# The expert stage of a two-layer decoder: transposed residual, Strassen's scheme for the first and last products, routing weights on h

## The chip, the cores and the metric

The kernel runs on one core of a Trainium2 chip. The metric is the device time of one execution in microseconds (us). Engines: TensorE (PE; its weight loads are PEld), VectorE (DVE), ScalarE (ACT), GpSimd (POOL) and SyncE (SP, which issues most of the DMAs).

## The reference, cut to what matters

The decoder has two layers of attention, cross-attention and feed-forward on 8 x 112 = 896 tokens of width 512. The change lies in the last stage, the feed-forward of the second layer, two rounds of experts on the normalized stream:

```python
res = xt                                   # 896 x 512, after the layer norm
for j in range(2):
    gate = xt @ Wg[j] + bg[j]              # 8 gates; the 6 largest count
    w = softmax(where(in_top, gate, -inf))
    h = einsum('th,nhe->nte', xt, Wup) + bup        # 6 experts, 512 -> 256
    h = silu(einsum('nte,nef->ntf', h, Wsw) + bsw) * h
    eo = einsum('nte,neh->nth', h, Wdn) + bdn       # 256 -> 512
    out = einsum('nth,tn->th', eo, w[:, :6])
    sh = (xt @ Wsu + bsu).reshape(-1, 2, 256)       # 2 shared experts
    sh = silu(sh @ Wsa + bsa) * sh
    out = out + sh.reshape(-1, 512) @ Wsd + bsd
    xt = res + out
return x + xt
```

The weights are the same in both rounds; only the gates differ. All is float32.

## The kernel before, in words

The whole program is unrolled. TensorE's instructions stand in the order in which the code writes them (`manual_schedule`); the order on the other engines and on the DMA queues is worked out by a scheduler from priorities and modelled times, and each engine then takes its own queue in order, waiting on semaphores.

The stage is `ffn_1` (from L1307). The layer norm writes `res` (token tiles of 128 x 512); GpSimd adds `res` onto `x` (L1335), so that `x` already holds stream and residual. For each round `j` the seven token tiles are turned by TensorE (`turned_tile`, L314) into `xT`, two halves of 448 tokens with the features on the partitions. For each of eight experts `m` (0 and 1 the shared ones):

- `rise` (L1407), the first product: for two halves of tokens and two blocks of 128 outputs, four products over the 512 features into a PSUM bank of tag `mm`; ScalarE adds the bias into `h1` (L1417).
- `switch` (L1421), the middle product: two products a block, ScalarE's silu (L1433), and GpSimd's product with `h1` into `h` (L1434).
- `down` (L1436), the last product: for each of seven token tiles two products with tokens on the rows and all 512 outputs as columns, into a bank of tag `s`. VectorE then multiplies the PSUM tile by the token's routing weight and adds it to the running sum in one operation (L1447); for shared experts it only adds (L1445).

The order is written out: first product of expert m+1, middle product of m, last product of m−1. The gates (`route`, L1337) are woven between the products of the first experts; `weights` makes the routing weights on VectorE (L1355 to L1389), and `turn` (L1391) turns them, split in two parts for precision, for the product with the experts' last biases (`bd`), which joins the last product of expert 1. The last products of expert 7 in round 0 are woven with the turning of round 1's tiles. At the end each tile of `x` leaves as soon as its sum is complete (L1502).

PSUM has eight banks: two of tag `mm`, two pairs of tag `s` (`wide`), two of tag `t` (`turning`). `wpool` has six slots of 1 MB for weights, in turn used by all stages. Nearly all products go through one helper, `accumulate` (L233), so they carry its line, L235; the tile's name tells them apart (`pf` for the first and the middle product, `po` for the last).

Of the kernel before, what the change touches and what calls it, by code (L numbers as in the profile page):

```python
# [27 lines left out]
_CONSTS = {}  # L28


def _constants():
# [28 lines left out]
    def rows(a):  # L60
# [7 lines left out]
        "ident": np.eye(P, dtype=f),  # L68
        **rope(0, e0, 64),
# [3 lines left out]
        "before": before,  # L73
# [82 lines left out]
def decoder(ctx: ExitStack, tc: tile.TileContext, i: dict, out: bass.AP):  # L156
# [32 lines left out]
    consts = cpool.tile([P, i["consts"].shape[1]], F32, name="consts")  # L189
    nc.scalar.dma_start(out=consts[:, :P], in_=i["consts"][:, :P])  # L190
# [8 lines left out]
    nc.sync.dma_start(out=consts[:, P:], in_=i["consts"][:, P:])  # L199
    first.append(weight(i["a_kv"][1], "wv0"))  # L200
    rspans, n = _spans(_ROWS)
    rows = cpool.tile([P, n], F32, name="rows")
    nc.sync.dma_start(out=rows, in_=i["rows"].partition_broadcast(P))

    def const(name, parts=P):
        at, n = _CONSTS[name]
        return consts[:parts, at : at + n]
# [12 lines left out]
    ctxT = cpool.tile([P, NB, T], F32, name="ctxT")  # L220
# [1086 lines left out]
    def ffn_1():  # L1307
        with (
# [3 lines left out]
            res = rpool.tile([P, NT, D], F32, tag="res", bufs=1, name="res")  # L1312
            nxt = rpool.tile([P, NT, D], F32, tag="nxt", bufs=1, name="nxt")
            up = [weight(i["f_up"][g], f"fup_{g}") for g in (3, 0, 1, 2)]
            dn = [weight(i["f_dn"][g], f"fdn_{g}", *((pool, "dn", 2) if g in (1, 2) else ())) for g in (3, 0, 1, 2)]
            sw = pool.tile([P, 7, 2, 256], F32, tag="sw", bufs=1, name="sw")
            nc.sync.dma_start(out=sw.rearrange("p a b c -> p (a b c)"), in_=i["f_sw"])
            wg = rpool.tile([P, 2, NC, 8], F32, tag="wg", bufs=1, name="wg")
            nc.sync.dma_start(out=wg.rearrange("p a b c -> p (a b c)"), in_=i["f_g"])


            b4 = pool.tile([P, D], F32, tag="b4", bufs=1, name="b4")
# [7 lines left out]
            nc.gpsimd.memset(w4, 0.0)  # L1330
            for tiles in GROUPS:
                layernorm([x[:, k, :] for k in tiles], [res[:, k, :] for k in tiles], eps5, f"ff1_{tiles[0]}", stats_behind[0])
            for k in range(NT):
                with tc.issue_after(spread[0]):
                    nc.gpsimd.tensor_tensor(x[:, k, :], x[:, k, :], res[:, k, :], ALU.add)  # L1335

            def route(j, xT, kept):  # L1337


                def gates(k):  # L1340
                    if k == 0:
                        kept["pg"] = turning(f"pgate_{j}")
                    pg = kept["pg"]

                    for hf in range(2):
                        lo, hi = max(k * P, hf * HT), min((k + 1) * P, (hf + 1) * HT)
                        if lo < hi:
                            accumulate(
                                pg[lo - k * P : hi - k * P, 8 * k : 8 * k + 8],
                                [(xT[hf][:, c, lo - hf * HT : hi - hf * HT], wg[:, j, c, :]) for c in range(NC)],  # L1350
                            )
                    if k == NT - 1:
                        weights(pg)

                def weights(pg):  # L1355
# [3 lines left out]
                        row("bg", P)[:, 8 * j : 8 * j + 8].unsqueeze(1).to_broadcast([P, NT, 8]), ALU.add,  # L1359
# [24 lines left out]
                    kept["w"] = w  # L1384
                    top4 = rpool.tile([P, NT, 8], F32R, tag="top4", name=f"top4_{j}")
                    nc.vector.tensor_copy(top4, w)
                    for at in (0, 64):
                        nc.vector.tensor_copy(w4[:, :, at : at + 8], top4.bitcast(F32))
                        nc.vector.tensor_tensor(w4[:, :, at + 32 : at + 40], w, top4.bitcast(F32), ALU.subtract)  # L1389

                def turn():  # L1391
                    kept["wT"] = wT = rpool.tile([P, NT * P], F32R, tag="wT", bufs=1, name=f"wT_{j}")
                    for a, b in ((0, 4), (4, NT)):
                        pt = turning(f"pwT_{j}_{a}")
                        for k in range(a, b):
                            nc.tensor.transpose(pt[:, (k - a) * P : (k - a + 1) * P], w4[:, k, :], ident)
                        nc.scalar.copy(wT[:, a * P : b * P], pt[:, : (b - a) * P])

                return gates, turn

            def expert(j, m, xT, src, dst, kept):

                g, e, shared = m // 2, m % 2, m < 2
                nm = f"{j}_{m}"
                at, hs = {}, {}

                def rise(hf, between=lambda: None):  # L1407
                    if hf == 0:
                        at["h1"] = pool.tile([P, 2, NB * T], F32, tag="h1", name=f"h1_{nm}")
                    for c in range(2):  # L1410
                        if c:
# [3 lines left out]
                        accumulate(ps[:, :HT], [(up[g][:, k, col0 : col0 + P], xT[hf][:, k, :]) for k in range(NC)])  # L1415
                        bias = col("bsu", 2 * e + c) if shared else col("bup", 2 * (m - 2) + c)
                        nc.scalar.activation(  # L1417
                            at["h1"][:, c, hf * HT : (hf + 1) * HT], ps[:, :HT], AF.Identity, bias=bias
                        )

                def switch(hf):  # L1421
                    if hf == 0:
                        at["h3"] = pool.tile([P, 2, NB * T], F32, tag="h3", bufs=3, name=f"h3_{nm}")
                    tokens = slice(hf * HT, (hf + 1) * HT)
                    for c in range(2):
                        ps = mm(f"pf2_{nm}_{hf}_{c}")
                        wi = 6 if shared else m - 2
                        accumulate(
                            ps[:, :HT], [(sw[:, wi, k, c * P : (c + 1) * P], at["h1"][:, k, tokens]) for k in range(2)]
                        )  # L1430
                        s = rpool.tile([P, HT], F32, tag="silu", name=f"silu_{nm}_{hf}_{c}")
                        bias = col("bsa", c) if shared else col("bsw", 2 * (m - 2) + c)
                        nc.scalar.activation(s, ps[:, :HT], AF.Silu, bias=bias)  # L1433
                        nc.gpsimd.tensor_tensor(at["h3"][:, c, tokens], s, at["h1"][:, c, tokens], ALU.mult)  # L1434

                def down(k):  # L1436
                    po = wide(f"po_{nm}_{k}")[:, 0, :]
                    tokens = slice(k * P, (k + 1) * P)
                    pairs = [(at["h3"][:, c, tokens], dn[g][:, 2 * e + c, :]) for c in range(2)]
                    if m == 1:  # L1440
                        pairs.append((kept["wT"][:, tokens], bd))
                    accumulate(po, pairs)
                    d = dst[:, k, :]
                    if shared:
                        nc.vector.tensor_tensor(d, src[:, k, :] if m == 0 else d, po, ALU.add)  # L1445
                    else:
                        nc.vector.scalar_tensor_tensor(d, po, kept["w"][:, k, m - 2 : m - 1], d, ALU.mult, ALU.add)  # L1447

                return rise, switch, down

            with tc.manual_schedule(engines={mybir.EngineType.PE}):
                tail = []
                for j in range(2):
                    src, dst, base = (res, nxt, res) if j == 0 else (nxt, x, x)
                    xT, kept = new_halves(f"ff1_{j}"), {}
                    experts = [expert(j, m, xT, base, dst, kept) for m in range(8)]
                    gates, turn = route(j, xT, kept)

                    for k in range(NT):
                        if k + 2 < len(tail):  # L1460
                            tail[k + 2]()
                        turned_tile(src[:, k, :], xT, k, f"ff1_{j}")
                        if k == 4:
                            experts[0][0](0)

# [6 lines left out]

                    experts[0][0](1, gate)
                    gate()
                    for m in range(8):
                        rise, switch, down = experts[m]
                        if m + 1 < 8:
                            experts[m + 1][0](0, gate)
                            gate()
                            switch(0)  # L1480
                            gate()
                            experts[m + 1][0](1, gate)
                            gate()
                            switch(1)
                        else:
                            switch(0)
                            switch(1)
                        if m == 1:
                            turn()
                        if m:  # L1490
                            for k in range(NT):
                                experts[m - 1][2](k)
                    tail = [lambda k=k, d=experts[7][2]: d(k) for k in range(NT)]
                    for step in tail[: 2 if j == 0 else NT]:
                        step()

# [3 lines left out]
    flat = out.rearrange("b t d -> (b t) d")  # L1500
    for k in range(NT):
        nc.sync.dma_start(out=flat[k * P : (k + 1) * P, :], in_=x[:, k, :])  # L1502
# [17 lines left out]
```

## Time and profile before

| | |
|---|---|
| runs | 1851.69, 1850.88, 1850.89 us; median 1850.89 |
| span of the profiled execution | 1850.4 us (no other time of that execution is given) |
| expert stage's products | from 1341.3 to 1846.0 us |
| busy: PE, PEld | 1809.1 (98%), 979.2 us |
| busy: DVE, ACT, POOL | 784.2 (42%), 658.1, 591.4 us |
| granted TensorE clock | 0.999 |
| DMA | 108.68 MB in all |

The page gives busy times as shares of the whole span. A matmul row's mean is the time of one record on its own; records overlap, so the pace is read from the chain or the timeline, where merged pieces show a start, a length and a count. A float32 product is two records. `min/median/max` on a single line's answer is in ns. Of the page's forty slices the last eleven hold the expert stage; in them VectorE is one to three tenths busy.

### The profile page before, as it was taken

To read this page: it belongs to the slowest core of one execution; us is meant where nothing else is said; L and a number is where in the kernel's file an instruction comes from. 1 tells how busy PE (TensorE), PEld (TensorE's weight loads), DVE (VectorE), ACT (ScalarE), POOL (GpSimd) and SP (SyncE) were. 2 spreads that over 40 slices of the span, in tenths; PEclk is the share of its full clock that TensorE was granted. 3 is DMA by queue.
4 is the path that set the end of the run, shared out by engine and by line. 5 is a ranking of instruction groups with operands and counts; after the bars stand their busy time and mean duration, and the time that the engine had idled before them with its cause. 6 is when DMAs were issued, how large, how long until landed. Compare 5 with 4: busy or idle time off the path is not lost.

```text
span 1850.4 us, 19741 instructions
## 1 busy us (share of the span) xinstructions
PE 1809.1 (98%) x7088; PEld 979.2 (53%) x7088; DVE 784.2 (42%) x1382; ACT 658.1 (36%) x1954; POOL 591.4 (32%) x520
## 2 busy tenths in 40 slices
PE   8999999999999999999999999999999999999999
PEld 4454544545554555677655555545554444554444
DVE  5455666655454545786432323336811112121213
ACT  2444344454333334565232322347632111121120
POOL 3455555355556530000233443302411011021111
PEclk9999999999999999999999999999999999999999
DMA  6132423043242212021212121301020000000001
GB/s 238 26 121 77 129 84 127 18 148 109 51 137 54 50 40 91 24 91 46 88 42 71 38 83 26 139 0 47 24 87 0 1 0 0 0 1 0 1 0 40
DMA packets 35497, 108.68 MB, mean 59 GB/s; under 512 B 6644, under 2 KB 20012, under 8 KB 28744
## 3 DMA queue, kind: packets, MB, share of 16 engines
q1 hardware_dynamic: 28264, 77.97, 13.0%
q0 software_dynamic: 6848, 29.36, 5.3%
q8 instruction: 56, 0.92, 0.2%
q14 instruction: 41, 0.34, 0.1%
q10 hardware_dynamic: 288, 0.09, 0.0%
HBM read 78.83 MB, written 10.22 MB: 48 GB/s over the span
## 4 chain that ended last, share of the span: by engine, by line
PE 89%; DVE 6%; ACT 3%; DMA 1%; SPq 1%; issue 0%; POOL 0%; POOLq 0%; DVEq 0%; ACTq 0%
PE pf L235 16%; PE po L235 11%; PE pr_q L235 10%; PE po_at L370 5%; PE po_at L374 5%; PE po_x L852 4%; PE pv L235 3%; PE ps L619 3%; PE po L637 3%; PE pr_k L235 3%; PE po_x L370 2%; PE pq_x L235 2%; PE po_x L374 2%; PE ps_x L816 2%; PE po_ff L1093 2%; PE ph L235 2%
## 5 line engine op out<-in xcount | busy, mean ns | idle before, releaser
L235 PE MATMUL pr_q<-xT_at,wq 128*128 128x448 f32 x512 | 204.1, 543 | 0.0
L1434 POOL TENSOR_TENSOR h<-silu,h 128x448 f32<-128x448 f32 x64 | 72.8, 1137 | 408.4 <-ACT silu L1433 408.4
L235 PE MATMUL pf<-xT_ff,fup 128*128 128x448 f32 x512 | 199.8, 541 | 1.6 <-ACT xT_ff L322 1.6
L235 PE MATMUL po<-fdn,h 128*128 128x512 f32 x448 | 197.2, 592 | 0.0
L235 PEld LDWEIGHTS pf<-xT_ff,fup 128*128 128x128 f32 x512 | 96.0, 190 | 93.0 <-issue 87.2
L404 POOL TENSOR_TENSOR p<-p,total 112x896 f32<-112x896 f32 (+1 forms) x56 | 85.4, 1531 | 179.4 <-DVE total L400 150.1
L1417 ACT ACTIVATE h<-pf,cols 128x448 f32<-128x448 f32 x64 | 40.6, 634 | 280.7 <-PE pf L235 278.2
L235 PEld LDWEIGHTS pr_q<-xT_at,wq 128*128 128x128 f32 x512 | 93.5, 190 | 84.6 <-issue 78.7
L235 PEld LDWEIGHTS po<-fdn,h 128*128 128x128 f32 x448 | 84.6, 190 | 100.6 <-issue 100.1
L397 ACT ACTIVATE p<-p,nmax 112x113 f32<-112x113 f32 x256 | 95.8, 376 | 109.2 <-DVE nmax L394 108.5
L370 PE MATMUL po_at<-wo,oT 128*128 128x512 f32 x224 | 109.9, 613 | 0.0
L374 PE MATMUL po_at<-wo,oT 128*128 128x512 f32 x224 | 105.3, 592 | 0.0
L235 PE MATMUL pf<-h,sw 128*128 128x448 f32 x256 | 101.5, 540 | 0.0
L567 POOL TENSOR_TENSOR qT<-qT,turned_q 128x448 f32<-128x448 f32 x64 | 75.6, 1185 | 53.9 <-DVE turned_q L566 47.4
L975 POOL TENSOR_SCALAR tl<-tr,ternary_bounds 128x512 f32<-128x512 f32 x32 | 51.8, 1617 | 122.8 <-DMA tr<-in_c_w_dram 122.8
L852 PE MATMUL po_x<-pT_x,kv 125*128 125x448 f32 x192 | 89.3, 549 | 1.7 <-DVE pT_x L847 1.4
L822 DVE TENSOR_REDUCE nmax_x<-ps_x 112x2 f32<-112x750 f32 x64 | 57.1, 933 | 79.5 <-PE ps_x L816 79.5
L565 POOL TENSOR_TENSOR qT<-raw_q,consts 128x448 f32<-128x448 f32 x64 | 79.7, 1251 | 26.1 <-ACT raw_q L556 18.7
L824 ACT ACTIVATE p_x<-ps_x,nmax_x 112x375 f32<-112x375 f32 x124 | 69.8, 575 | 38.2 <-DVE nmax_x L822 38.1
L416 DVE COPY pT<-ppt 112x448 f32<-112x448 f32 x96 | 57.0, 615 | 61.0 <-PE ppt L415 60.9
L1447 DVE SCALAR_TENSOR_TENSOR nxt<-po,wr,nxt 128x512 f32<-128x512 f32 x42 | 31.5, 751 | 120.6 <-PE po L235 120.6
L1447 DVE SCALAR_TENSOR_TENSOR x<-po,wr,x 128x512 f32<-128x512 f32 x42 | 31.5, 751 | 118.8 <-PE po L235 118.8
(255 smaller groups left out, 3189.1 us busy)
## 6 DMA issues: line engine op xcount, KB each, us to landing
tw<-in_c_w_dram SPq DMA_DIRECT2D x16, 512.0 KB
tr<-in_c_w_dram POOLq DMA_DIRECT2D x32, 256.0 KB, 4.1
signs<-tl POOLq DMA_DIRECT2D x32, 256.0 KB, 2.9
turned_q<-raw_q SPq DMA_DIRECT2D x128, 56.0 KB
turned_q<-raw_q SPq DMA_DIRECT2D x64, 112.0 KB
wq<-in_a_q_dram SPq DMA_DIRECT2D x4, 1024.0 KB
wo<-in_a_o_dram SPq DMA_DIRECT2D x4, 1024.0 KB
bq<-in_b_q_dram SPq DMA_DIRECT2D x4, 1024.0 KB
```

The lines of the kernel that those rows point to most:

```text
L235: nc.tensor.matmul(ps, lhsT, rhs, start=(k == 0), stop=(k == len(pairs) - 1))
L370: nc.tensor.matmul(ps[0], lhsT, rhs, start=(c == 0), stop=False)
L374: nc.tensor.matmul(ps[0], lhsT, rhs, start=False, stop=(c == len(pairs) - 1))
L397: nc.scalar.activation(p[:, h, :], src[:, h, :], AF.Exp, bias=nmax[:, h : h + 1], accum_out=total[:, h : h + 1])
L404: spread[:] = [nc.gpsimd.tensor_tensor(p[:, at, :T], p[:, at, :T], total[:, at], ALU.mult).ins]
L565: nc.gpsimd.tensor_tensor(by_batch(dst), by_batch(raw), cos, ALU.mult)
L567: nc.gpsimd.tensor_tensor(dst, dst, turned, ALU.add)
L822: nc.vector.tensor_reduce(nmax, ps[:T, :, :L], AX.X, ALU.max, negate=True)
L824: e = nc.scalar.activation(p[:, 2 * j + s, :], ps[:T, s, :L], AF.Exp, bias=nmax[:, s : s + 1], accum_out=total[:, 2 * j + s : 2 * j + s + 1],)
L852: nc.tensor.matmul(po[0][:, : 4 * T], kv[:, b, c, :], pTs[c], start=(c == 0), stop=(c == NLC - 1))
L1434: nc.gpsimd.tensor_tensor(at["h3"][:, c, tokens], s, at["h1"][:, c, tokens], ALU.mult)
L1447: nc.vector.scalar_tensor_tensor(d, po, kept["w"][:, k, m - 2 : m - 1], d, ALU.mult, ALU.add)
```

## The change

All of it is for the last stage, with some room made for it.

**Transposed residual.** The running sum is no longer kept with tokens on the rows but turned, as two halves `acc` of [features, 448 tokens]. In round 0 it starts from `xT`; round 1 takes it as its `xT` without turning anything, and sums into a new one. At the end `leaving` turns it back, adds it to `x` and sends the tile out.

**Seven block products for eight.** First and last products are cut 2 x 2 x 2: the summed dimension, the outputs and the tokens each in two. `quad` makes the four output blocks from seven block products (two products of 128 x 128 by 448 each) in the order 1, 6, 7, 2, 5, 4, 3. Products 1 and 2 share a bank, 6, 5 and 3 another, 7 and 4 a third; after each product the engine named in `after` reads the bank as it then is. The operands need sums: of the weights (`summed`, four GpSimd operations for a 1 MB block, into a slot of `wpool`), of the tokens (`xs`, four VectorE operations a round) and of h (four VectorE operations an expert, which turn `h3`'s four blocks into seven). Expert 0 keeps the plain form. Since `summed` writes into the weight block, weights are loaded in each round.

**Routing weights on h.** With the sum turned, a token's weight is no longer a scalar of a partition. `turn` also writes the turned weights to DRAM (`gated`), `share` reads each expert's row back onto all partitions, and VectorE multiplies the blocks of h by it (not for shared experts). The bias product is a step of its own, `begin`.

**Order.** Step `s` weaves the first product of expert s+1 with the middle product of s; from step 2 on, a call of the last product for a pair of experts follows (half of the outputs in each). Gates come earlier: all seven are done in step 0, and `turn` is at its end.

**Room.** Constants and rows not needed in this stage, and `ctxT`, move to a pool `early`, released before it. The middle weights are loaded per expert (`gating`), `res` lies in two slots of `wpool`.

```diff
+            def summed(engine, name, a11, a12, a21, a22):
+                ...
+                engine.tensor_tensor(s1, a21, a22, ALU.add)
+                engine.tensor_tensor(a21, a11, a21, ALU.subtract)
+                engine.tensor_tensor(s2, s1, a11, ALU.subtract)
+                engine.tensor_tensor(s4, a12, s2, ALU.subtract)
+                return s1, s2, s4
+            def quad(products, after, name):
+                bank = {}
+                def step(n):
+                    if n == 1:
+                        bank[1] = bank[2] = mm(f"pa_{name}")[:, :HT]
+                    if n == 6:
+                        pair = wide(f"pb_{name}")
+                        bank[6] = bank[5] = bank[3] = pair[:, 0, :HT]
+                        bank[7] = bank[4] = pair[:, 1, :HT]
+                    pairs = list(zip(*products()[n]))
+                    for k, (lhsT, rhs) in enumerate(pairs):
+                        nc.tensor.matmul(
+                            bank[n], lhsT, rhs, start=(k == 0 and n in (1, 6, 7)),
+                            stop=(k == len(pairs) - 1), skip_group_check=True,
+                        )
+                    after[n](bank[n])
+                return [lambda n=n: step(n) for n in (1, 6, 7, 2, 5, 4, 3)]
 ...
                 def turn():
+                        nc.scalar.copy(plain[:, a * P : b * P], pt[:16, : (b - a) * P])
                         nc.scalar.copy(wT[:, a * P : b * P], pt[:, : (b - a) * P])
+                    nc.sync.dma_start(out=gated[j], in_=plain[8:16, :])
+                def share(e):
+                    kept["share", e] = t = pool.tile([P, NB * T], F32, tag="share", name=f"share_{j}_{e}")
+                    nc.sync.dma_start(out=t, in_=gated[j, e : e + 1, :].partition_broadcast(P))
 ...
+                def rise():
+                    ...
+                    after = {
+                        1: first, 6: begun(0), 7: begun(1),
+                        2: lambda ps: nc.scalar.activation(h(0, 0), ps, AF.Identity, bias=bias[0]),
+                        5: more(1, 1), 4: more(1, 0), 3: more(0, 1),
+                    }
 ...
+                        nc.scalar.activation(s, ps[:, :HT], AF.Silu, bias=b)
+                        to = h3[:, 2 * c + hf]
+                        nc.gpsimd.tensor_tensor(to, s, at["h1"][:, c, half(hf)], ALU.mult)
+                        if not shared:
+                            nc.vector.tensor_tensor(to, to, kept["share", m - 2][:, half(hf)], ALU.mult)
+                        if (hf, c) == (1, 1):
+                            nc.vector.tensor_tensor(h3[:, 5], h3[:, 3], h3[:, 1], ALU.subtract)
+                            nc.vector.tensor_tensor(h3[:, 1], h3[:, 1], h3[:, 0], ALU.subtract)
+                            nc.vector.tensor_tensor(h3[:, 4], h3[:, 3], h3[:, 1], ALU.subtract)
+                            nc.vector.tensor_tensor(h3[:, 6], h3[:, 2], h3[:, 4], ALU.subtract)
 ...
+            def begin(j, base, acc, kept):
+                def one(hf, f):
+                    ps = turning(f"pbd_{j}_{hf}_{f}")
+                    nc.tensor.matmul(ps[:, :HT], bd[:, f * P : (f + 1) * P], kept["wT"][:, hf * HT : (hf + 1) * HT], ...)
+                    if base is None:
+                        nc.scalar.copy(acc[hf][:, f], ps[:, :HT])
+                    else:
+                        nc.vector.tensor_tensor(acc[hf][:, f], base[hf][:, f], ps[:, :HT], ALU.add)
 ...
+            def down(j, q, f, experts, acc):
+                ...
+                def first(ps):
+                    kept["r"] = pool.tile([P, HT], F32, tag="first", name=f"first_{j}_{q}_{f}")
+                    nc.scalar.copy(kept["r"], ps)
+                    plus(nc.gpsimd, 0, 1, kept["r"])
+                def sixth(ps):
+                    plus(nc.vector, 1, 0, ps)
+                    plus(nc.gpsimd, 1, 0, kept["r"])
+                def fifth(ps):
+                    plus(nc.vector, 1, 1, ps)
+                    plus(nc.gpsimd, 1, 1, kept["r"])
+                ...
 ...
+                    for s in range(8):
+                        up = experts[s + 1][1]() if s < 7 else []
+                        sw_steps = experts[s][2]()
+                        for kind, nxt, k in loads.get(s, ()):
+                            load(kind, j + nxt, k)
+                        if 1 <= s < 7:
+                            share(s - 1)
+                        gating(j + (s == 7), (s + 1) % 8)
+                        for k in range(max(len(up), 4)):
+                            if k < len(up):
+                                up[k]()
+                            if k < 4:
+                                sw_steps[k]()
+                                if s == 0:
+                                    gate()
+                        if s == 0:
+                            turn()
+                        if s == 1:
+                            run([(0, f) for f in begin(j, base, acc, kept)])
+                        if s >= 2:
+                            for step in down(j, (s - 2) // 2, s % 2, experts, acc):
+                                step()
+                    for step in down(j, 3, 0, experts, acc):
+                        step()
+                    last = down(j, 3, 1, experts, acc)
+                    for k, step in enumerate(last):
+                        step()
+                        if j:
+                            leaving(0, k, acc)
+                for k in range(NT):
+                    leaving(1, k, acc)
```

## The prediction

> **What bounds the kernel now.** I read the page first (shares, then the chain), then the chain in order of time over the last stage, then single lines of VectorE and GpSimd.
>
> ```profile
> PE 1809.1 (98%) x7088; PEld 979.2 (53%) x7088; DVE 784.2 (42%) x1382; ACT 658.1 (36%) x1954; POOL 591.4 (32%) x520
> ...
> PE 89%; DVE 6%; ACT 3%; DMA 1%; SPq 1%; issue 0%; POOL 0%; POOLq 0%; DVEq 0%; ACTq 0%
> ```
>
> TensorE is busy for 98% of the span and is 89% of the chain that ended last. VectorE and GpSimd hold 6% and nothing of it. The expert stage lies at the end, and there the chain is almost nothing but products:
>
> ```profile
> 1376.61 21.20 PE pf L235 x56
> 1397.81 0.77 PE pwT L1396 x7
> 1398.57 12.02 PE po L235 x28
> 1410.59 18.04 PE pf L235 x48
> 1428.63 13.64 PE po L235 x35
> ...
> 1590.42 1.72 PE po L235 x4
> 1592.14 0.44 PE pt_ff L318 x4
> ...
> 1600.79 0.64 ACT h L1417
> 1601.42 0.97 ACT xT_ff L322 x2
> 1602.39 0.04 issue
> ...
> 1821.93 24.05 PE po L235 x56
> 1846.00 0.75 DVE x L1447
> ```
>
> Each float32 product is two records. The `pf` rows (448 columns) give 18.04/48 = 0.3758 us a record; the `po` rows (512 columns) 12.02/28 = 0.4293. A record of 448 columns lasts 539 ns alone, but the next starts after 376: what counts is the pace. The clock is 0.999. The price list of the other engines, from single lines (minimum/median/maximum in ns):
>
> ```profile
> L566 DVE TENSOR_TENSOR turned_q<-turned_q,consts x64: 612/625/3157, 24.0 to 1181.3; 128x448 f32<-128x448 f32 x64
> ...
> L297 DVE TENSOR_SCALAR res<-x,mv_ff,rstd_ff x7: 517/546/1495, 1331.4 to 1340.4; 128x512 f32<-128x512 f32 x7
> ...
> L1335 POOL TENSOR_TENSOR x<-x,res x7: 1254/1448/1510, 1332.0 to 1341.4; 128x512 f32<-128x512 f32 x7
> ...
> L1434 POOL TENSOR_TENSOR h<-silu,h x64: 1127/1131/1347, 1367.3 to 1822.7; 128x448 f32<-128x448 f32 x64
> ...
> L375 DVE TENSOR_TENSOR x<-x,po_at x56: 673/687/690, 78.7 to 1249.6; 128x512 f32<-128x512 f32 x56
> ```
>
> The reader is to see that L566 and L297 (all operands in SBUF) have maxima far above their medians, and that L375, with one operand in PSUM, has not. L297 and L1335 run at the same time, the one behind the other.
>
> **The sum.** It is made against the profile's span, 1850.4; the median of the runs is 1850.89, so 0.5 is added at the end.
>
> *Up products.* Seven of eight experts a layer go from 16 to 14 products: 2 x 2 records x 7 experts x 2 layers = 56 records less, x 0.3758 = −21.0.
>
> *Down products.* Their count stays: 8 experts x 7 tiles x 2 = 112 a layer before, 8 calls x 7 products x 2 = 112 after. The gain is the width, 448 columns for 512: 448 records x (0.4293 − 0.3758) = −24.0. The middle products (`sw`) stay.
>
> *Transposed residual.* The second layer needs no turning: 7 x 0.44 = 3.1 and the wait for ScalarE at 1600.79, 0.64 + 0.97 + 0.04 = 1.65: −4.7. Turning back at the end is 32 products of 0.11; the half inside the last call costs +1.8, the other half lies in the tail. The bias product cost (13.64 − 12.02)/7 = 0.231 a tile; 8 of 448 columns at 0.20 for 7: nothing.
>
> TensorE's own sum: −21.0 − 24.0 − 4.7 + 1.8 = −47.9.
>
> *Tail.* From the last product to the end it was 1850.4 − 1846.0 = 4.4, since six of seven output tiles had already left, 1.72 apart. Now every tile leaves only after its second half: VectorE's additions of 256 columns (a 128x256 copy out of PSUM at L714 took 0.42, so 0.45) end 0.2 + 0.69 (the read of the last product) + 8 x 0.45 = 4.5 after it, and from VectorE's last end to the span's end there were 1850.4 − 1846.75 = 3.65. So 8.1 for 4.4; the seven transfers (1.84 MB; a stretch at 1341 moved 407 GB/s, so 4.5 us) fit beside it. +4 (3 to 7).
>
> *Turn of the routing weights.* The last gate is now in step 0, with five products (7.5 us) between it and the transposes; before there were 21.20. VectorE's chain from the gates to `w4` ran 6.05 alone (1376.46 to 1382.5), one more copy is 0.2, and in between it must read three PSUM blocks (0.65 each) and make up to four differences of h (0.62): 8.2 to 10.7, so 1 to 3 of wait a layer. I take 2: +4 (0 to 10).
>
> *`begin`.* Eight products of 0.20 through two banks, each emptied in 0.62 and a hand-over of 0.1: 8 x 0.7 = 5.6 less 1.6 less the last two, not waited for: about 2.8 a layer, +5.5 (0 to 8). `pgate` now holds one of the two `mm` banks, so step 0's first product waits for ScalarE's read (0.2 + 0.63): +1.8 (0 to 2).
>
> *Hidden work.* A full step (up call, switch, down call) is 14 + 8 + 14 = 36 float32 products, 72 records x 0.376 = 27.1 us. In it VectorE has 5 + 8 + 6 = 19 operations at 0.62 to 0.75, 12 us, where it had 7 x 0.75; GpSimd 4 + 3 at 1.13 and on most steps a weight sum of four at 1.3 to 1.45, together 13.4 (views with steps like those of the sums are in no row; at twice L1335's price it would be 19); ScalarE 7 x 0.63 = 4.4. All have room, so their sums cost nothing. Sixteen weight loads of 1 MB for eight go into slots freed a step or more ahead of their first use, and a load of that size landed in 5.0 to 5.2 us (`wk`, `wv`, `wq`, `wo` in the list of DMA issues): nothing. SyncE queues them among the `share` and `sw` loads, each needed a whole step later: nothing; if that cover went, a late weight would cost its 5 us once. At the start, five slots of the six suffice beside the last output weight for the two `normal` blocks: nothing.
>
> *The wait that is new.* In a call the products run 1, 6, 7, 2, 5, 4, 3, and 5 and 3 add into 6's bank: product 3 waits until VectorE has read 5, with only 4 (1.5 us) between. A reader gets a product 0.2 after its pace ends (the eight records begun at 1341.15 end theirs at 1344.16, and ScalarE starts on them at 1344.36); VectorE needs 0.69 (L375) and some 0.05 back: slack 0.56. What stands before it in VectorE's queue counts. In the up half these are `to *= share` and the four differences of h, both with all operands in SBUF, which can be held up by a GpSimd operation: L566's 625 against 1336 for the worst of `turned_k`, L297's 546 against 1495 say 0.7 to 0.95 for one. One difference behind one GpSimd operation in front of the read is 0.62 + 0.95 − 0.56 = 1.0 late. The ends: nothing (a wait can't give a gain), or that in all 30 calls, 30. By the timing of a step (the differences start some 2.9 after the last switch product ends, the read of 5 is due at 1.7) the reading mostly comes first; I take half of it in the 14 up calls and 0.15 in the 16 down calls: 7 + 2.4 = +9 (0 to 30). Behind the late read wait VectorE's later reads; TensorE waits for those a call later at the earliest.
>
> A rule of the Trainium skill stands here against the change. SBUF — State Buffer, section "SBUF: two separate sides", says that a VectorE operation with two SBUF inputs and a GpSimd operation that reads SBUF lock each other out for a whole instruction. L297 and L566 agree with a full block (0.7 to 0.95 and more on top), and L375's 690 agrees that a PSUM input escapes it. By the rule taken at its worst, eight differences and share products a step, each behind a whole GpSimd operation of 1.13, VectorE's 12 us would be 21 of a step's 27: still below TensorE, but with a read late in most calls, and the sum would end near the upper end, +30 for +9.
>
> Sum: −47.9 + 4 + 4 + 5.5 + 1.8 + 9 = −23.6. 1850.4 − 23.6 + 0.5 = 1827.3.
>
> **The rivals.**
>
> *All hidden.* VectorE always comes in time, and the turn too: −47.9 + 4 (tail) + 1.8 (bank) + 2 (of `begin`, whose banks are sure to be late) = −40; 1811. For it: before, TensorE waited 0.8 us in all after 1450. Against: that stage had 7 VectorE operations an expert and none that TensorE needed within 1.5 us.
>
> *Slower: VectorE stands behind a weight sum.* VectorE's queue is in order; if `to *= share` waits for GpSimd's h, and that stands behind a weight sum of four operations (4 x 1.385 = 5.5), the read of product 5 is up to 5.5 − 0.56 = 4.9 late. Fifteen sums fall among products. Without my +9 the change brings −32.6, so it decides from the seventh full collision on (7 x 4.9 = 34); at ten it is 49 − 32.6 = +16.4: 1867. For it: GpSimd is half busy and each sum also waits for a load. Against: the queues' order need not put the sum first, and up calls have switch products that stretch the other gaps to 3 us.
>
> *Eaten up.* Nearly every call pays the 1.0 and the turn its 10: −47.9 + 4 + 10 + 8 + 2 + 24 = 0; 1851. Seven products for eight would then be what the page counts, and not what the time shows.
>
> **How the numbers follow.** Forecast 0.62, all hidden 0.17, behind a sum 0.15, eaten up 0.06 (half of it still faster, half the same). This kernel's measurement can tell about 0.2%, 3.7 us. Faster 0.62 + 0.17 + 0.03 = 0.82; same 0.03; slower 0.15. The forecast's own band is 1815 to 1843, from its bounds; the range reaches down to all of TensorE's sum with the tail only (−47.9 + 4 = −43.9: 1807) and up to just short of eaten up, 1849; it leaves out the slow rival and the edge of the last.
>
> **What would show it.** Right: about 56 fewer records of 448 columns in the up products, down records 0.376 apart; TensorE's idle time small and found before `turn`, in `begin`, and before third products, with VectorE as releaser; some 8 us from the last product to the end. Wrong: idle TensorE of over 1 us in every call, with VectorE's reads held by GpSimd (behind a sum); VectorE's SBUF operations at 1.3 us and more as a rule; a longer start of the stage; or a pace of records above 0.376 with operands from the summed weights.

## The result, and the profile after

The changed kernel takes 1945.67 us, median of four runs (1943.73 to 1946.66), against 1850.89 (1850.64 to 1851.69): a ratio of 1.051, 95% interval 1.0495 to 1.0525. The forecast was 1827.3 in a range of 1807 to 1849: it has the wrong sign. The profiled execution has a span of 1944.9 us and a granted clock of 0.991.

From the page of the changed kernel, the busy times and the shares of the chain that ended last:

```profile
PE 1807.2 (93%) x7042; PEld 969.8 (50%) x7042; DVE 910.3 (47%) x1580; ACT 649.7 (33%) x1946; POOL 724.9 (37%) x634
...
PE 78%; DVE 10%; issue 3%; ACT 3%; POOL 3%; DMA 2%; SPq 1%; ACTq 0%; DVEq 0%; POOLq 0%
```

TensorE is as long busy as before (1809.1), but for 93% of a longer span and not 98%; VectorE's part of the chain went from 6% to 10%, and GpSimd's from nothing to 3%. Busy time misleads here: a record whose successor comes late counts with its full length of 0.54 us, where one that the next overlaps adds only its pace of 0.376, and at half clock a record counts for more still. So the starts were counted instead. Each record of the stage was given its undisturbed pace (0.3758 us for 448 columns, 0.4293 for 512, the small ones theirs) and the rest of the distance to the next start was put down as lost. Before, the stage had 502.0 us of pace and 2.3 lost. Now it has 457.7 and 139.4. TensorE's own gain of 44.3 is there; 137 us of new idle time stand against it.

Where they lie shows in a single call of the last product. The chain in order of time (start, length, what), changed kernel; `pa` is the tile of products 1 and 2, `pb` that of 6, 5, 3 and of 7, 4:

```profile
1461.97 1.50 PE pa_dn L1401 x4
1463.47 1.52 PE pb_dn L1401 x4
1464.99 0.02 issue
1465.02 0.63 DVE acc L1623
1465.65 0.04 issue
1465.69 1.77 PE pb_dn L1401 x4
1467.46 1.50 PE pa_dn L1401 x4
1468.97 1.52 PE pb_dn L1401 x4
...
1470.51 0.63 DVE acc L1623
...
1471.18 1.78 PE pb_dn L1401 x4
```

Read it as 1, 6, then VectorE's read of 6, then 7; then 2, 5, VectorE's read of 5, then 4. Products 7 and 4 have a bank of their own, which nobody is reading at that time, and still they start only when the read of the other bank has ended: 0.63 of VectorE and two hand-overs, 0.71 of idle time in the timeline and 0.87 by the starts, on a product of 1.5. Product 3 then waits for the read of 4 in the same way. In the trace the weight load that opens product 7 waits for the semaphore that VectorE raises with this read, so the wait is one that the program holds. Three of seven products stand at VectorE's pace in the down calls, although VectorE was not late: in the chain it begins each of the two reads shown 0.02 to 0.03 after the product's last record.

The groups of TensorE's instructions of the stage (busy, mean ns of one, idle time just before them and what ended it):

```profile
L1401 PE MATMUL pb_dn<-h,sums_dn 128*128 128x448 f32 x192 | 81.8, 549 | 12.3 <-DVE acc L1623 6.3 <-DVE xT_ff L1623 6.0
L1401 PE MATMUL pb_dn<-h,fdn 128*128 128x448 f32 x128 | 58.9, 584 | 28.0 <-DVE acc L1623 14.2 <-DVE xT_ff L1623 13.8
...
L1401 PE MATMUL pb_up<-xs,fup 128*128 128x448 f32 x112 | 54.9, 617 | 39.4 <-DVE h L1559 20.1 <-DVE h L1554 16.5 <-DVE wr L1496 2.8
```

The weights `fdn` with `pb_dn`, and `fup` with `pb_up` and `xs`, are products 7 and 4. By the starts they lost 33.2 us in the down calls and 43.3 in the up calls; product 3 lost 15.0 and 14.4. That is 105.9 of the 139.4, in 86 waits.

In the up calls the wait is longer, since there VectorE's reads stand in a queue behind work that waits for GpSimd. The chain of the same kernel, at one of four places where product 7 waited 3.8 to 3.9:

```profile
1473.03 4.73 DMA fup<-in_f_up_dram
...
1477.89 1.27 POOL sums_up L1335
1479.23 1.26 POOL fup L1336
1480.50 1.22 POOL sums_up L1337
1481.72 1.10 POOL h L1584
...
1484.43 0.68 DVE h L1554
...
1485.15 3.27 PE pb_up L1401 x4
```

A weight block lands at 1477.76; GpSimd takes three operations of its sum ahead of the block of h (L1584), though ScalarE had that block's silu done at 1479.24; VectorE's `share` product (L1586) waits for h, takes 1.67 by the timeline, beside the fourth operation of the sum, and only then reads product 6; and product 7, four records long, takes 3.27 where it took 1.77 elsewhere. The table of stretches explains the last (us, PE, PEld, DVE, ACT, POOL busy, granted clock, DMA share and GB/s):

```profile
1485.00:1488.20 3.20, 3.05 (x4) 1.52 (x5) 0.72 (x2) 0.00 (x0) 0.49 (x1) 0.50 0.00 0
1488.20:1491.00 2.80, 2.80 (x9) 1.45 (x8) 0.68 (x1) 0.63 (x1) 0.27 (x1) 1.00 0.00 0
```

At the end of that wait and behind it the clock was at half, over the whole first stretch of 3.2 us. Behind the six waits over 3.6 us (by the starts: these four, and one in the down call of step 7 of each round, at 1600.00 and 1894.17) 34 records started 0.37 to 0.53 late, about 13 us in all.

### The profile page after: what moved, and what is told of

It is laid out like the page before. It is cut to its first block, busy times and chain, and to the rows that moved or that the text cites. A ratio compares the mean times of both kernels' runs of the same rounds, so it can differ in the third digit from the quotient of the medians.

```text
span 1944.9 us, 19991 instructions
## 1 busy us (share of the span) xinstructions
PE 1807.2 (93%) x7042; PEld 969.8 (50%) x7042; DVE 910.3 (47%) x1580; ACT 649.7 (33%) x1946; POOL 724.9 (37%) x634
## 4 chain that ended last, share of the span: by engine, by line
PE 78%; DVE 10%; issue 3%; ACT 3%; POOL 3%; DMA 2%; SPq 1%; ACTq 0%; DVEq 0%; POOLq 0%
PE pr_q L244 9%; PE pb_dn L1401 6%; PE pf L244 5%; PE po_at L379 5%; PE po_at L383 5%; PE po_x L861 3%; PE pb_up L1401 3%; PE pv L244 3%; PE ps L628 3%; PE po L646 3%; PE pr_k L244 3%; PE pa_dn L1401 2%; PE po_x L379 2%; PE pq_x L244 2%; PE po_x L383 2%
## 5 line engine op out<-in xcount | busy, mean ns | idle before, releaser
L1584 POOL TENSOR_TENSOR h<-silu,h 128x448 f32<-128x448 f32 x64 | 75.4, 1180 | 183.9 <-ACT silu L1582 183.7
L244 PE MATMUL pf<-h,sw 128*128 128x448 f32 x256 | 109.3, 555 | 0.0
L1586 DVE TENSOR_TENSOR h<-h,share 128x448 f32<-128x448 f32 x48 | 36.0, 750 | 133.3 <-POOL h L1584 133.3
L1401 PE MATMUL pb_dn<-h,sums_dn 128*128 128x448 f32 x192 | 81.8, 549 | 12.3 <-DVE acc L1623 6.3
L1401 PE MATMUL pb_up<-xs,fup 128*128 128x448 f32 x112 | 54.9, 617 | 39.4 <-DVE h L1559 20.1
L1582 ACT ACTIVATE silu<-pf,cols 128x448 f32<-128x448 f32 x64 | 40.5, 633 | 151.7 <-PE pf L244 151.6
L574 POOL TENSOR_TENSOR qT<-raw_q,tables 128x448 f32<-128x448 f32 x64 | 78.0, 1223 | 25.5 <-ACT raw_q L565 18.8
L1401 PE MATMUL pb_dn<-h,fdn 128*128 128x448 f32 x128 | 58.9, 584 | 28.0 <-DVE acc L1623 14.2
L384 DVE TENSOR_TENSOR x<-x,po_at 128x512 f32<-128x512 f32 x56 | 38.5, 687 | 91.3 <-PE po_at L383 91.0
L244 PEld LDWEIGHTS pf<-h,sw 128*128 128x128 f32 x256 | 50.6, 197 | 50.6 <-issue 46.5
```

The source lines that it names most:

```text
L244: nc.tensor.matmul(ps, lhsT, rhs, start=(k == 0), stop=(k == len(pairs) - 1))
L574: nc.gpsimd.tensor_tensor(by_batch(dst), by_batch(raw), cos, ALU.mult)
L1401: nc.tensor.matmul(bank[n], lhsT, rhs, start=(k == 0 and n in (1, 6, 7)), stop=(k == len(pairs) - 1), skip_group_check=True,)
L1584: nc.gpsimd.tensor_tensor(to, s, at["h1"][:, c, half(hf)], ALU.mult)
```

## The experiments

Theory A, the shared tile: the program makes a product wait for the last reader of its *tile*. Products 6, 5, 3 and 7, 4 write two banks of one tile `pair`, so each of them waits for VectorE's read of the one before. Theory B, late readers: VectorE comes late because it stands behind GpSimd's sums of weights, wherever the products are put.

**A tile of its own for products 7 and 4.** Nothing else is touched; `wide` still gives two banks, of which each tile uses one.

```diff
-                        pair = wide(f"pb_{name}")
-                        bank[6] = bank[5] = bank[3] = pair[:, 0, :HT]
-                        bank[7] = bank[4] = pair[:, 1, :HT]
+                        bank[6] = bank[5] = bank[3] = wide(f"pb_{name}")[:, 0, :HT]
+                    if n == 7:
+                        bank[7] = bank[4] = wide(f"pc_{name}")[:, 0, :HT]
```

> The banks of products 6, 5, 3 and of 7, 4 become two tiles instead of the two halves of one; nothing else changes. Theory A (products wait for each other's readers because both banks belong to one tile: 7 for the read of 6, 4 for the read of 5, 3 for the read of 4): in the down calls three waits of about 0.9 each vanish, some 41 us of the 48 that stand there; in the up calls the 1.84 before product 4 goes and the 0.8 to 1.8 before product 3 shrinks to a few tenths, some 33 of 58: 1870 us (1860 to 1885). Theory B (VectorE and GpSimd come late whatever the tiles; the waits move to products 5 and 3): 1925 or more.

Measured: 1828.97 (1824.82 to 1830.63), ratio to the kernel before 0.9876, 0.9862 to 0.9891. It is 116.7 less than the changed kernel and further down than A foresaw. The page and the chain of this kernel, `pc` being the new tile:

```profile
PE 1773.3 (97%) x7042; PEld 967.0 (53%) x7042; DVE 909.0 (50%) x1580; ACT 649.8 (36%) x1946; POOL 722.9 (40%) x634
```

```profile
1472.03 1.50 PE pa_dn L1401 x4
1473.54 1.50 PE pb_dn L1401 x4
1475.04 1.50 PE pc_dn L1401 x4
1476.54 1.50 PE pa_dn L1401 x4
1478.05 1.50 PE pb_dn L1401 x4
1479.55 1.50 PE pc_dn L1401 x4
1481.05 1.50 PE pb_dn L1401 x4
```

The same seven products in 10.5 us with nothing between them. Lost time in the stage falls from 139.4 to 19.9. Why it fell further than expected: the queue in front of VectorE's read of 6 is still there, four times in the stage, but product 7 no longer waits for it; all that is left of it is 0.2 to 0.3 more before product 3. At the first of these places the timeline of this kernel (start, length, instruction) has:

```profile
1460.54 1.67 DVE L1586 TENSOR_TENSOR h<-h,share 128x448 f32<-128x448 f32 x1 [5.18 <-POOL h L1584]
1460.55 1.67 PE L1401 MATMUL pc_up<-xs,fup 128*128 128x448 f32 x4
...
1462.13 0.67 DVE L1554 SCALAR_TENSOR_TENSOR h<-pb_up,delta,h 128x448 f32<-128x448 f32 x1
```

Product 7 starts at 1460.55, and product 6 is read only from 1462.13 on. The long waits go, and in this profiled execution the half clock with them (0.999); the other three of this kernel had a granted clock of 0.996 to 0.997 and took 3 to 6 us more.

**The sums of weights later.** The shared tile stays; each sum is put behind the step's last GpSimd product of h, which is B's cure.

```diff
-                    kept[j, g].prepare()
+                    behind.append(kept[j, g].prepare)
 ...
+                        for prepare in sums:
+                            with tc.issue_after(gated_h[0]):
+                                prepare()
```

> The weight sums of a step stand behind the step's last GpSimd product of h, where they now stand in front of or between these products; the shared tile stays. Theory A: only the four long waits (3.8 to 3.9 before product 7 of an up call) and the halved clock after them go, about 6.5 each: 1920 us (1912 to 1932). Theory B (GpSimd's sums in front of h are the main cost): 1880 or less.

Measured: 1989.01 (1988.38 to 1989.64), ratio 1.0744, 1.0723 to 1.0766: 43 more than the changed kernel, where less was expected. The long waits before product 7 of the up calls did go (from 3.9 at most to 0.7), but the sums now run beside the four differences of h, and the waits are back before 4 and 3. One of them, in the groups of VectorE, changed kernel:

```profile
L1589 DVE TENSOR_TENSOR h<-h 128x448 f32<-128x448 f32 x16 | 10.0, 625 | 0.5
```

and with the sums late:

```profile
L1589 DVE TENSOR_TENSOR h<-h 128x448 f32<-128x448 f32 x16 | 20.5, 1282 | 0.5
```

L1588 and L1590 went from 620 and 624 to 1155 and 1213. They stand ahead of the reads of 5 and 4. A product 4 and the product 3 behind it in TensorE's timeline of this kernel:

```profile
1467.40 1.77 PE L1401 MATMUL pb_up<-xs,fup 128*128 128x448 f32 x4 [2.72 <-DVE h L1559]
1472.31 2.86 PE L1401 MATMUL pb_up<-xT_ff,sums_up 128*128 128x448 f32 x4 [3.14 <-DVE h L1559]
```

By the starts product 4 of the up calls now waits up to 2.9 us (35.6 in all, where it was 25.2) and product 3 up to 5.8 (40.9 in all, where it was 14.4). With the gain at product 7 the waits of 7, 4 and 3 grow by 23 us; the rest of the 43 was not taken apart, but the granted clock fell from 0.991 to 0.976. Neither theory foresaw this: what the place of the sums costs hangs on what they stand beside.

**Both edits.**

> Both edits. Theory A: the two add up, 1945.7 - 75 - 28: 1842 us (1830 to 1855), so faster than the kernel before by some 0.5%. Theory B: near the kernel with late sums alone.

Measured: 1848.66 (1847.15 to 1853.89, ten runs), ratio 0.9987, 0.9978 to 0.9997. Late sums cost the split kernel 19.7 as well; product 3 of the up calls loses 15.0 where it lost 5.6. B's cure harms with either form of the tile, and it does not bring the time back; A's does so by itself. That the time lies in A's range is luck: the two terms that A added, -75 and -28, were -116.7 and +43.

**Eight products for eight.** First and last products plain, without sums and differences; transposed residual, `begin`, `turn` and the weights on h as in the changed kernel.

```diff
-                return quad(lambda: falls[j, order[q]].products(f, h3()), after, f"dn_{j}_{q}_{f}")
+                def block(h, hf):
+                    ps = wide(f"pb_dn_{j}_{q}_{f}_{h}_{hf}")[:, 0, :HT]
+                    ...
+                    plus(nc.vector, h, hf, ps)
+                return [lambda h=h, hf=hf: block(h, hf) for h in range(2) for hf in range(2)]
```

> The transposed residual, the routing weights on h and begin stay, but first and last products are eight for eight: no sums of weights, of tokens or of h, four blocks of four products in each call. Theory A: TensorE's own work is that of before less the turning (-3), and the fixed costs begin (+5.8), the bank held by the gates (+1.8) and the tail (+4) are left: 1858 us (1850 to 1868). Theory B (the transposed residual itself is what costs, through share, begin or the weight loads): 1880 or more.

Measured: 1869.79 (1869.25 to 1870.32), ratio 1.01, 1.008 to 1.012: 2 us above A's range, and well short of B's 1880. The stage has 502.8 of pace, as before the change (502.0), and 20.0 lost. So seven products for eight are worth 40.8 in time against the split kernel (45.1 in pace: 120 records of 0.3758), and what surrounds them costs 18.8 against the kernel before.

**The tile split in the down calls alone, and in the up calls alone.**

```diff
+                        apart = name.startswith("dn")     # "up" in the other kernel
 ...
+                        bank[7] = bank[4] = wide(f"pc_{name}")[:, 0, :HT] if apart else first[:, 1, :HT]
```

> Two tiles for the two banks in the last products' calls alone; the first products keep the shared one. Theory A (each call pays for its own shared tile): the 48 us of waits in the down calls go but for 1.4, and some 5 of halved clock after the longest of them: 1945.7 - 52 = 1894 (1885 to 1905). Theory C (the queues' order, which the scheduler changes with the tiles, did most of it): no fixed share; far from 1894, and the two halves do not add up to the 117 of the full split.

> The reverse: two tiles in the first products' calls alone. Theory A: of their 57.8 us of waits 5.6 are left, and about 12 of halved clock go with the four long ones: 1945.7 - 64 = 1881 (1870 to 1892). Theory C as for the other half.

Measured: 1882.17 (1882.16 and 1882.17) and 1882.76 (1880.93 and 1884.59), ratios 1.017 (1.0149 to 1.019) and 1.0173 (1.0153 to 1.0193). Each half gives 63 us; for the down calls that is more than expected (the lower end was 1885), for the up calls it is what was expected. The lost time of the other kind of call stays: 33.2 and 15.0 in the down calls of the second kernel, as in the changed one. The two sum to 126.4 for 116.7: with the down calls split, the four long waits of the up calls come to 2.3 each for 3.8 to 3.9, so some 6 of these 10 are counted twice; the rest is not settled.

**The split tile without sums of weights.** GpSimd's sums are left out.

```diff
-                engine.tensor_tensor(s1, a21, a22, ALU.add)
-                ...
-                return s1, s2, s4
+                return a11, a22, a12
```

> Two tiles, and the four GpSimd sums of each weight block are left out (the products take blocks that are not summed, so the output is another). Theory A (with two tiles a late read of product 6 reaches no product, so the sums on GpSimd and their hold on VectorE's SBUF operations are hidden): 1826 us (1821 to 1831), within 0.3% of the split kernel's 1829. Theory B (GpSimd's sums cost on their own): 1815 or less.

Measured: 1828.52 (1827.15 to 1829.1), the same as with them (1828.97). Where they stood, the sums are free once the tile is split.

**The split tile, `begin` woven.** Two of its products go behind each of the last three products of the up call of step 1, where no middle product follows.

```diff
+                            elif starts:
+                                run([(0, f) for f in starts[:2]])
+                                del starts[:2]
```

> Two tiles, and begin's eight products stand two behind each of the last three products of step 1's up call and two after them, where they stood in a row. Their 6.1 us of waits for two banks shrink to about 1.5: 1824.5 us (1821 to 1829). If VectorE's queue then brings the third product's read late instead, no change.

Measured: 1827.0 (1824.44 to 1827.41), ratio 0.9869, 0.9854 to 0.9883. The waits of `begin` fall from 6.1 to 4.7, but the time can't be told from that of the split tile alone. Both beat the kernel before and the changed kernel.

## Why the prediction was wrong

The step that failed is "the wait that is new". It said: "product 3 waits until VectorE has read 5, with only 4 (1.5 us) between", since "5 and 3 add into 6's bank". I counted the waits by the bank that a product writes, and nothing at all for 7 and 4. The code that I had before me makes both banks halves of one tile `pair`, and the waits follow the tile: 7 waits for the read of 6, 4 for that of 5, 3 for that of 4, with no product between but for a middle product before 7 in the up calls. In place of a slack of 0.56 there is none: of 86 waits (by the starts) most cost 0.87 to 0.97, though the reader came at once; late readers make it 1.5 to 3.9; only with the middle product between is it as little as 0.4. The term of 9 became 105.9, and about 13 for the half clock that the longest bring. The two kernels that split the tile in one kind of call each show it in both kinds.

The upper bound went with it. "Nothing, or that in all 30 calls, 30" bounded the lateness of one read, and never asked whether more than one product waits. The range was too narrow for that reason, not for a badly chosen duration. Of the sign that I named, "idle TensorE of over 1 us in every call, with VectorE's reads held by GpSimd (behind a sum)", the first half is what the profile shows. The second holds for four calls of 30; in the down calls the reads mostly came at once.

The rest of the sum can be held against the split kernel, in which the waits do go by bank, as I took them:

- TensorE's own sum, −47.9: from the first record to the end of the last product the stage took 504.8 before (1341.15 to 1846.0) and 473.7 in the split kernel (1339.68 to 1813.35), −31.1; less what was lost in it (17.6 there, 2.3 before) that is −46.4. Of the −47.9, 1.65 was a wait and counts among those 2.3; the rest, −46.3, is what was measured.
- `begin` +5.5: 6.1. The bank of `pgate` +1.8: 2.0. The turn +4: 0.4; VectorE's chain came through in time, and this term was too large.
- Product 3, +9 (7 up and 2.4 down): 5.6 in the up calls; in the down calls nothing before product 3, and 1.4 before product 5, which waits for the read of 6 in the same bank.
- The tail +4: from the end of the last product to the span's end it is 9.7 (1813.35 to 1823.0) where it was 4.4, so +5.3.
- Together −25.6 where I had −23.6; the profiled execution gives 1823.0 − 1850.4 = −27.4, 1.5 of it before the stage (its first record is at 1339.68, before the change at 1341.15). That execution was the shortest of its four, at 1824.82. By the medians it is 1828.97 against my 1827.3: these terms held for another kernel than the one that I was shown. That they come so close is partly luck, since the turn, 3.6 too large, and product 3, 2.0 too large, make up for the smaller errors of the others.

The hidden work was rightly put at nothing as long as no product hangs on a read that it delays: without the sums the split kernel is no faster. The rival "VectorE stands behind a weight sum" had a real mechanism and the wrong place. The sum does come first four times (the waits of 3.8 to 3.9), but product 7 pays for it and not product 3, and only because of the shared tile. By itself it would not have made the kernel slower: the split kernel has four such collisions too, at 0.2 to 0.3 us each. "All hidden" and "eaten up" both assumed the waits by bank and fall with them.

The rule in SBUF — State Buffer, section "SBUF: two separate sides", of the Trainium skill spoke against this change, and I took the milder value. The runs agree with the rule: a difference with two SBUF inputs (L1589) took 1282 ns on average in the kernel that puts GpSimd's sums beside it, and 625 in the changed kernel, whose sums stand elsewhere. There the two seldom met; where they were made to meet, the kernels took 43 and 20 us more.

## What to carry to other kernels

Before a wait is priced, list for each instruction all that the program makes it wait for, by the unit in which the program tracks it: two banks in one tile are one thing to wait for, and results that take turns in such a tile come no faster than their readers. When a chain of products goes from no reader within its slack to a reader after each product, multiply the hand-over (0.87 us here by the starts) by the number of products first, and argue about late readers only then. And a cure that moves work on one engine is judged by what will run beside it: once the tile was split, GpSimd's sums were free in front of h, and beside the differences they cost 20 us.

## What the runs showed of the hardware

The half clock came behind shorter waits than I had thought. With the tile split in the down calls only, a line of TensorE's timeline and the stretches behind it:

```profile
1478.31 3.01 PE L1405 MATMUL pb_up<-xs,fup 128*128 128x448 f32 x4 [2.11 <-DVE h L1558]
```

```profile
1478.30:1479.40 1.10, 1.09 (x2) 0.64 (x3) 0.00 (x0) 0.00 (x0) 1.02 (x2) 0.68 0.00 0
1479.40:1482.00 2.60, 2.60 (x5) 1.16 (x4) 0.75 (x2) 0.00 (x0) 1.82 (x2) 0.50 0.00 0
```

An idle time of 2.11 us was followed by half clock from 1478.7 on, 0.4 us after TensorE had begun again, for 3.4 us (the 0.68 of the first stretch is full clock up to 1478.7 and half clock behind it). Three of the four waits of 2.3 (by the starts) in that kernel were, and each made four or five records 0.37 later; none of the fourteen waits of 1.82 to 1.84 (by the starts) in the changed kernel was. TensorE: Matmul & The Clock Gate, Part 1, "The HAM clock gate (the "warmup" mystery)", of the Trainium skill gives an idle window of about 3.4 us for the drop to half rate: the waits of 3.6 agree, those of 2.1 to 2.2 (idle time by the trace) came sooner, and here the measurement decides.

The clock's record in the traces shows why three waits did and the fourth did not. In each profiled execution the stretches at half clock begin on one grid of steps of 3.413 us, and those that end before the program does last one, two or three steps. Take a step of the expert stage at full clock, and count how much of it TensorE's records fill, at 0.84 ns a column (0.3758 us for 448): of 1478 such steps in the ten kernels, all 36 that were filled to less than 36% were followed by half clock, none of the 1437 filled to more than 38% was, and of the five between, two. So as far as these traces show it is the share of a step that counts, and a wait that lies across the border of two steps, as the fourth does, can go without it.
